# The tail of a two-layer convolution block: column sums moved between two matmuls, three loads moved earlier, two more load buffers

## The chip, the cores and the metric

The kernel runs on one core of a Trainium2 chip. The metric is the device time of a run in microseconds, the median of three timed runs. A profile of one more execution shows what each engine did: PE (matmuls; PEld is its weight load), DVE (vector work), ACT (activations), POOL (general work, and here also the issue of all indirect loads), SP (issue of most other transfers), and the 16 DMA engines that move the data for all queues.

## The reference

The input `x` is an image of 512 x 512 positions with 64 channels. Two layers are added to it, one after the other:

```
x = x + L0(group_norm(x))   # layer norm, gated triangular product over a mask, layer norm, output gate
x = x + L1(group_norm(x))   # 12 x 12 lowest Fourier modes, mixed over channels, transformed back
```

Only the end matters here. `group_norm` takes mean and variance over the whole image for 32 groups of two channels. `L1` needs the Fourier sums of the whole image at 12 x 12 modes; the norm's scale and shift are applied to the modes. Then, at each mode, a 64 x 64 complex matrix mixes the channels, and the inverse transform is added to every position. So nothing of the output can be finished before the last position of the first layer has been seen.

## The kernel before, in words

Only the path for a mask with at most 256 set rows (`compact`) runs. Rows are sorted so that masked ones stand together.

**The unit loop** (line 1047 on) makes the first layer's output `x1`. It goes over 32 units, each 32 columns x 256 rows of the image (two blocks r of 128 rows) in a buffer of 4096 values per partition (`place(i)`, a slice of the big tile `places`). Each unit has 8 steps n; in them PE transposes, centers and projects, DVE scales (`z_t`) and takes group statistics (`statistics`, L1023, into `stats2c`), ACT does sigmoids and squares, and POOL multiplies by the gate's partner (`gated`, L974) and adds to the input (`added`, L978). POOL also issues the loads of units to come (`load`, through `gather`, L628). All is emitted in this order by hand; each engine takes its instructions in the order of emission. The unit's results go to memory through SP (`store`, L994, to the halves `x1_h`, named `x_h` in the profile), its column sums go through `transform` and `save` (L1017) to `modes_d`. In the last unit but one SP issues the loads of the mixing weights `w_real` and `w_imag` (L1141) into `wide`, a part of `places`. The last quarter of the last unit is finished by DVE (`finished`) instead of POOL.

**Between the loops**, in order of emission: POOL clears `picks` (L1160), loads the last 128 rows of `modes_d` (`fetch(3)`, L893, into `modes_t`), and issues the loads of the first `AHEAD` = 13 tiles of `x1` (`fetch_rows`, L628). A tile is 128 rows x 32 columns x 64 channels, 1 MB; there are 64. Ten of the 13 buffers are parts of `places` that have come free, three are tiles `lx_t`. Then `group_norm_affine` computes scale and shift: a reduction on DVE, the matmul `mean_ps` (L253), four DVE steps up to `v`, the matmul `var_ps` (L265), and a chain of small DVE steps (`rsqrt` and what follows) up to `ab2`. After it `columns(3)` runs 12 matmuls `t_ps` (L888) over `modes_t` and adds the result to `sums` (L889). Then come `turned` (L1174), the writing of `picks`, the mixing matmuls `mixed_ps` (L1192), which read `picks` and `wide`, and the first `back_columns` (`q_ps`, `it_ps`), which makes a quarter of the inverse column transform.

**The last loop** (line 1246 on) takes the 64 tiles in order: four matmul groups `l_ps` (L1254), four additions on DVE (L1261), a store to the output through SP (L1262), and the load of the tile `AHEAD` places on into the same buffer, which waits until that store has landed. Three more `back_columns` are spread over it.

Of the kernel before, what the change touches and what calls it, by code (L numbers as in the profile page):

```python
# [9 lines left out]
F32 = mybir.dt.float32  # L10
# [7 lines left out]
P = 128  # L18
N = 512
C = 64  # L20
# [6 lines left out]
MODES = 12  # L27
M2 = 2 * MODES
EPS = 1e-5
JC = 32  # L30
NJ = N // JC
K = 2 * P
AHEAD = 13
SHARE = 22
QB = 4

# [10 lines left out]
def conv_preact_kernel(ctx: ExitStack, tc: tile.TileContext, t: dict):  # L47
# [190 lines left out]
        nc.vector.tensor_reduce(between, means, AX.X, ALU.add)  # L238
        nc.vector.scalar_tensor_tensor(var, var, 1.0 / count, between, ALU.mult, ALU.add)

    def group_norm_affine(keep, sets, each, name):


        groups, n = sets[0].shape[1:]
        avg = avg_p if groups == G else avg_c
        ab = keep.tile([P, 3], F32, name="ab_" + name)
        with tc.tile_pool(name="gn_" + name, bufs=1) as gp, tc.tile_pool(
            name="gnp_" + name, bufs=1, space=PSUM
        ) as gps:
            part = gp.tile([P, groups], F32, name="part")  # L250
            nc.vector.tensor_reduce(part, sets[0], AX.X, ALU.add)
            mean_ps = gps.tile([P, groups], F32, name="mean_ps")
            nc.tensor.matmul(mean_ps, avg, part, start=True, stop=True)  # L253
            mean = gp.tile([P, groups], F32, name="mean")
            nc.vector.tensor_scalar(mean, mean_ps, 1.0 / (n * each), None, ALU.mult)
            d = gp.tile([P, groups, n], F32, name="gn_d")
            nc.vector.scalar_tensor_tensor(
                d, sets[0], 1.0 / each, mean.unsqueeze(2).to_broadcast([P, groups, n]), ALU.mult, ALU.subtract
            )
            nc.vector.tensor_mul(d, d, d)  # L260
            nc.vector.scalar_tensor_tensor(d, sets[1], 1.0 / each, d, ALU.mult, ALU.add)
            v = gp.tile([P, groups], F32, name="v")
            nc.vector.tensor_reduce(v, d, AX.X, ALU.add)
            var_ps = gps.tile([P, groups], F32, name="var_ps")
            nc.tensor.matmul(var_ps, avg, v, start=True, stop=True)  # L265
            rs = rsqrt(gp, var_ps, 1.0 / n, EPS, [P, groups])
            if groups == G:
                mine = gp.tile([P, 2, G], F32, name="mine")
                nc.vector.tensor_mul(mine[:, 0, :], rs, pick)
                nc.vector.tensor_mul(mine[:, 1, :], mean, pick)  # L270
                am = gp.tile([P, 2], F32, name="am")
                nc.vector.tensor_reduce(am, mine, AX.X, ALU.add)
                rs, mean = am[:, 0:1], am[:, 1:2]
            nc.vector.scalar_tensor_tensor(ab[:, 1:2], mean, -1.0, rs, ALU.mult, ALU.mult)
            nc.vector.tensor_copy(ab[:, 0:1], rs)
            nc.vector.tensor_scalar(ab[:, 2:3], mean, -1.0, None, ALU.mult)
        return ab
# [334 lines left out]
    def compact(fc):  # L612
# [193 lines left out]
        with tc.tile_pool(name="tri", bufs=1) as trp:  # L806
# [57 lines left out]
            with tc.manual_schedule(), tc.tile_pool(name="late", bufs=1) as lp:  # L864
# [15 lines left out]
                parts = wide.rearrange("p a b -> p (a b)").rearrange("p (k f) -> p k f", k=2)  # L880
                modes_t = places[:, 7 * 64 * C : 7 * 64 * C + M2 * C].rearrange("p (m c) -> p m c", c=C)

                def columns(h, pool):
                    by = modes_t.rearrange("p (m k) c -> p m (k c)", k=2)
                    ps = pool.tile([P, 4, P], F32, name="t_ps").rearrange("p i k -> p (i k)")[:, : MODES * M2]
                    ps = ps.rearrange("p (m n) -> p m n", m=MODES)
                    for m in range(MODES):
                        nc.tensor.matmul(ps[:, m, :], by[:, m, :], col_basis[:, h, :], start=True, stop=True)  # L888
                    nc.vector.tensor_add(sums, sums, ps)  # L889

                def fetch(h):

                    (nc.gpsimd if h == 3 else nc.sync).dma_start(modes_t, modes_d[h * P : (h + 1) * P])  # L893

                with tc.tile_pool(name="np_x", bufs=LEAD + 2) as tp, tc.tile_pool(name="np_q", bufs=2) as sqp, tc.tile_pool(
                    name="np_s", bufs=3
# [150 lines left out]
                    for s in range(-LEAD, total_g + 2 * SIZE):  # L1047
# [94 lines left out]

                with tc.tile_pool(name="lq", bufs=1) as qp, tc.tile_pool(name="lx", bufs=1) as xp:

                    free = 3 * 64 * C + C * MODES * MODES
                    buffers = [places[:, free : free + JC * C].rearrange("p (n c) -> p n c", c=C)]
                    buffers += [place(i)[:, r * JC : (r + 1) * JC] for i in (6, 2, 0, 1) for r in range(2)]
                    buffers += [place(7)[:, JC:]]
                    buffers += [xp.tile([P, JC, C], F32, name=f"lx_t{i}") for i in range(AHEAD - len(buffers))]
                    ranked = [h.rearrange("s (k j) c -> (s k) (j c)", k=NJ // 2) for h in x1_h]  # L1150
                    tiles_left = [(jc, b) for jc in range(NJ) for b in range(4)]
                    xts = {}

                    def fetch_rows(jc, b):
                        xts[jc, b] = buffers[(4 * jc + b) % AHEAD]
                        gather(xts[jc, b].rearrange("p j c -> p (j c)"), ranked[jc // 8], dst_i, b, jc % 8)


                    picks = qp.tile([P, MODES, MODES, 32], F32, name="picks")
                    nc.gpsimd.memset(picks, 0.0)  # L1160
                    fetch(3)
                    for jb in tiles_left[:AHEAD]:
                        fetch_rows(*jb)
                    rinv = qp.tile([P, 4, P], F32, name="rinv")
                    nc.scalar.dma_start(rinv, t["c_rinv"])
                    col_inv = qp.tile([P, 2, 4, P], F32, name="col_inv")
                    nc.scalar.dma_start(col_inv, t["c_col_inv"])
                    ab2 = group_norm_affine(lp, sets, 8, "x1c")
                    with tc.tile_pool(name="tcp", bufs=1, space=PSUM) as tcp:
                        columns(3, tcp)  # L1170
                    with tc.tile_pool(name="sps", bufs=1, space=PSUM) as sps:

                        turned = sps.tile([P, MODES, M2], F32, name="turned")
                        nc.tensor.matmul(  # L1174
                            turned.rearrange("p m n -> p (m n)"), turn, sums.rearrange("p m n -> p (m n)"), start=True, stop=True
                        )
                        v = qp.tile([P, 2, MODES, MODES], F32, name="v_modes")
                        nc.vector.tensor_add(v[:, 0], sums[:, :, :MODES], turned[:, :, MODES:])
                        nc.vector.tensor_sub(v[:, 1], turned[:, :, :MODES], sums[:, :, MODES:])
                        for k in range(2):  # L1180
                            to = picks.rearrange("p m n k -> p m (n k)")[:, :, 12 * k : 12 * k + 33 * 11 + 1 : 33]
                            nc.vector.tensor_scalar(to, v[:, k], ab2[:, 0:1], None, ALU.mult)
                            h = slice(k * C, (k + 1) * C)
                            one = picks[h, 0, 0, 12 * k : 12 * k + 1]
                            nc.vector.scalar_tensor_tensor(one, ab2[h, 1:2], float(N * N), one, ALU.mult, ALU.add)

                        mixed_ps = sps.tile([P, 3, C], F32, name="mixed_ps")
                        for m3 in range(3):
# [54 lines left out]
                    with tc.tile_pool(name="lpq", bufs=1, space=PSUM) as pq, tc.tile_pool(  # L1243
                        name="lpt", bufs=2, space=PSUM
                    ) as pt, tc.tile_pool(name="lps", bufs=4, space=PSUM) as pp:
                        for jc in range(NJ):
                            for b in range(4):
                                it = parts[:, jc // 8, (jc % 8) * N : (jc % 8 + 1) * N]
                                xt = xts.pop((jc, b))
# [92 lines left out]
```

## Time and profile before

| | before |
|---|---|
| timed runs, us | 1892.57, 1892.95, 1894.03; median 1892.95 |
| the profiled execution: its own time, us | 1886.98 |
| its span, us | 1885.2 |
| busy in the span: PE, DVE, ACT, POOL | 89%, 77%, 49%, 46% |
| end of the statistics of the last unit, us | 1554.2 |
| end of the last mixing matmul, us | 1581.1 |
| DMA rate from 1602 to 1850 us | 425 GB/s |

Times in the text are counted from the start of the span. A line of a timeline gives the start, the time from there to the end of the group, the engine, the line of the kernel, the operation with its output and inputs, the number of instructions, and in brackets the idle time of the engine just before and what ended it. SPq, ACTq and POOLq are the issuing side of a queue. A line of the stretch table gives, for each stretch, its length, the busy time and the number of instructions of each engine, the granted TensorE clock as a share of full speed, the mean busy share of the DMA engines and the bytes that they moved per time. Shares slightly above 1 are an effect of how packets are counted into stretches.

### The profile page before, as it was taken

How to read it: one execution, taken by the hardware profiler on the slowest of the kernel's cores; microseconds unless marked ns; L12 is line 12 of the kernel's file. 1: busy time of each engine (PE TensorE's matmuls, PEld its weight loads, DVE VectorE, ACT ScalarE, POOL GpSimd, SP SyncE). 2: the span in 40 equal slices, each digit the busy share in tenths (PEclk: the TensorE clock that was granted, in tenths of full speed). 3: DMA queues.
4: the chain of work that ended last, by engine and by line, in shares of the span. 5: the costliest groups of instructions: out<-in, count | busy, mean ns of one | idle time of the engine just before them, and what ended most of it. 6: DMA issues, size and time to landing. Idle time of an engine off the chain costs nothing. (4 is left out here: it accounts for less than half of the span.)

```text
span 1885.2 us, 33737 instructions
## 1 busy us (share of the span) xinstructions
PE 1683.2 (89%) x11598; PEld 1350.9 (72%) x11598; DVE 1458.5 (77%) x2997; ACT 922.0 (49%) x1606; POOL 873.0 (46%) x678
## 2 busy tenths in 40 slices
PE   6779899998999999999999999999999956998873
PEld 5666666664788889998888888788888835664441
DVE  5989677777555568888999799979999994665552
ACT  3565555653222255567777677757767720111000
POOL 3655111111000000029999799979998982111110
PEclk9989899999999999999999899989999986555555
DMA  6999155556656534237777676767777589999999
GB/s 250 387 373 382 62 141 135 138 140 160 206 179 179 151 137 165 116 136 259 260 235 251 219 238 243 242 219 259 254 262 248 199 226 366 419 427 427 426 427 389
DMA packets 188868, 468.22 MB, mean 248 GB/s; under 512 B 35184, under 2 KB 134384, under 8 KB 147600
## 3 DMA queue, kind: packets, MB, share of 16 engines
q1 hardware_dynamic: 158192, 262.40, 41.4%
q0 software_dynamic: 27856, 202.19, 28.1%
q8 instruction: 94, 1.54, 0.3%
q10 hardware_dynamic: 2640, 1.38, 0.3%
q14 instruction: 86, 0.70, 0.1%
HBM read 278.13 MB, written 187.76 MB: 247 GB/s over the span
## 5 line engine op out<-in xcount | busy, mean ns | idle before, releaser
L934 PE MATMUL w_ps<-gate_x,xt_c 128*128 128x128 f32 x2048 | 281.9, 282 | 32.1 <-DVE z_t L1112 30.7
L978 POOL TENSOR_TENSOR places<-places,z_t 128x1024 f32<-128x1024 f32 x127 | 302.1, 2378 | 8.2
L934 PEld LDWEIGHTS w_ps<-gate_x,xt_c 128*128 128x128 f32 x2048 | 253.1, 195 | 49.1 <-DVE z_t L1112 48.6
L934 PE MATMUL c_ps<-center_x,xt_c 128*128 128x128 f32 x2048 | 276.3, 278 | 0.2
L934 PEld LDWEIGHTS c_ps<-center_x,xt_c 128*128 128x128 f32 x2048 | 252.5, 194 | 2.3 <-ACT xt_c L929 1.1
L944 ACT ACTIVATE sq_c<-c_ps 128x512 f32<-128x512 f32 x320 | 188.6, 590 | 104.3 <-PE c_ps L934 103.8
L1254 PE MATMUL l_ps<-places,rinv 24*128 24x512 f32 x512 | 209.7, 1128 | 31.7 <-DVE places L1261 25.7
L1112 DVE TENSOR_TENSOR z_t<-w_ps,rs_n 128x512 f32<-128x512 f32 x320 | 216.1, 675 | 23.0 <-PE w_ps L934 22.7
L1023 DVE BATCH_NORM_STATS2 stats2c<-places 128x6 f32<-128x128 f32 x1024 | 220.5, 279 | 8.1 <-POOL places L978 8.1
L948 DVE TENSOR_REDUCE scratch<-sq_c 128x16 f32<-128x1024 f32 x160 | 194.6, 1216 | 16.6 <-ACT sq_c L944 11.8
L1068 ACT ACTIVATE z_t<-z_t 128x1024 f32<-128x1024 f32 x128 | 135.5, 1058 | 142.0 <-DVE z_t L1115 117.7
L1115 DVE TENSOR_TENSOR z_t<-z_t,scratch 128x1024 f32<-128x1024 f32 x160 | 195.4, 1221 | 11.7 <-ACT rs_n L954 3.4
L1254 PEld LDWEIGHTS l_ps<-places,rinv 24*128 24x128 f32 x512 | 120.9, 304 | 115.4 <-DVE places L1261 73.1
L974 POOL TENSOR_TENSOR z_t<-z_t,bias_row_out 128x1024 f32<-128x1024 f32 x63 | 149.6, 2374 | 113.0 <-DMA places<-u_d 108.7
L924 PE MATMUL t_ps<-c_ident,places 128*128 128x128 f32 x1280 | 196.6, 277 | 1.3 <-DVE places L853 1.3
L1261 DVE TENSOR_TENSOR places<-places,l_ps 128x512 f32<-128x512 f32 x200 | 124.2, 683 | 86.5 <-DMA places<-x_h,dst_i 53.4
L929 ACT ACTIVATE xt_c<-t_ps,ab_xc 128x512 f32<-128x512 f32 x256 | 175.8, 687 | 23.8 <-PE t_ps L924 23.8
L924 PEld LDWEIGHTS t_ps<-c_ident,places 128*128 128x128 f32 x1280 | 148.9, 143 | 52.3 <-issue 52.3
L628 POOL DMA_INDIRECT places<-in_x,src_i x64 | 62.6, 978 | 261.9 <-PE c_ps L934 210.9
L974 POOL TENSOR_TENSOR z_t<-z_t,places 128x1024 f32<-128x1024 f32 x64 | 151.3, 2365 | 32.2 <-ACT z_t L1068 32.0
L678 DVE BATCH_NORM_STATS2 stats1c<-x_ps 128x6 f32<-128x512 f32 x256 | 156.0, 683 | 12.2 <-PE x_ps L677 11.3
L853 DVE SCALAR_TENSOR_TENSOR places<-tri_c_ps,slot_t,mask_s 128x256 f32<-128x256 f32 x128 | 73.1, 650 | 85.3 <-PE tri_c_ps L849 85.3
(203 smaller groups left out, 2641.9 us busy)
## 6 DMA issues: line engine op xcount, KB each, us to landing
x_h<-places SPq DMA_DIRECT2D x64, 1024.0 KB
out_x<-places SPq DMA_DIRECT2D x50, 1024.0 KB
places<-u_d SPq DMA_DIRECT2D x512, 64.0 KB
left_d<-o_c SPq DMA_DIRECT2D x64, 256.0 KB
right_d<-o_c SPq DMA_DIRECT2D x64, 256.0 KB
left_raw<-left_d SPq DMA_DIRECT2D x64, 256.0 KB
right_raw<-right_d SPq DMA_DIRECT2D x64, 256.0 KB
u_d<-z_t SPq DMA_DIRECT2D x32, 512.0 KB
```

The costliest lines, as they stand in the source:

```text
L678: nc.vector.bn_stats(stats[:, 0, 16 * (jc % quarter) + 4 * r + c, :], ps.rearrange("p i k -> p (i k)"))
L924: nc.tensor.transpose(tps[:, i, :], flat[:, o : o + P], ident)
L929: nc.scalar.activation(xts[s], tps, AF.Identity, bias=ab1[:, 2:3])
L934: nc.tensor.matmul(ps[:, 2 * i : 2 * i + 2, :], xts[s][:, i, :], w, start=True, stop=True)
L944: nc.scalar.activation(sqs[s // 2][:, 8 * (n % 2) : 8 * (n % 2) + 8, :], cps, AF.Square)
L948: nc.vector.tensor_reduce(totals[k % 2][:, 8 * (n - 1) : 8 * (n + 1)], sqs.pop(s // 2), AX.X, ALU.add)
L974: nc.gpsimd.tensor_mul(zs[k, c], zs[k, c], u)
L978: nc.gpsimd.tensor_add(xr, xr, zs.pop((k, c)))
L1023: nc.vector.bn_stats(st[k // 4][:, g, k % 4, :], x_of(k)[:, :, 2 * g : 2 * g + 2])
L1112: nc.vector.tensor_mul(z[:, 8 * odd : 8 * odd + 8, :], wps, rs)
L1115: nc.vector.tensor_add(z, z, bias.unsqueeze(1).to_broadcast([P, 16, C]))
L1254: nc.tensor.matmul(ps.rearrange("p j o -> p (j o)"), rinv[h, b, :], it[h], start=True, stop=True, tile_position=(32 * g, 0),)
```

## The change

It has three parts.

- `columns` is split into a list of steps. `group_norm_affine` gets a function `between`, which it calls after each of its two matmuls: seven of the twelve column matmuls are emitted right after `mean_ps`, five right after `var_ps`, and the addition to `sums` after the whole of `group_norm_affine`.
- The first three loads of the last loop's tiles are emitted inside the unit loop: one in the last unit but one at n = 3, two in the last unit at n = 3 and n = 6. There they stand on POOL after `gated` or `added` of that step.
- `AHEAD` is 15 instead of 13. The two added buffers are the memory of `picks`; their first loads are emitted after the mixing matmuls. The other ten of the first 13 loads stay where they were.

```diff
-AHEAD = 13
+AHEAD = 15
...
-    def group_norm_affine(keep, sets, each, name):
+    def group_norm_affine(keep, sets, each, name, between=lambda i: None):
...
             nc.tensor.matmul(mean_ps, avg, part, start=True, stop=True)
+            between(0)
...
             nc.tensor.matmul(var_ps, avg, v, start=True, stop=True)
+            between(1)
...
-                def columns(h, pool):
+                def column_sums(h, pool):
...
-                    for m in range(MODES):
-                        nc.tensor.matmul(ps[:, m, :], by[:, m, :], col_basis[:, h, :], start=True, stop=True)
-                    nc.vector.tensor_add(sums, sums, ps)
+                    steps = [
+                        lambda m=m: nc.tensor.matmul(ps[:, m, :], by[:, m, :], col_basis[:, h, :], start=True, stop=True)
+                        for m in range(MODES)
+                    ]
+                    return steps + [lambda: nc.vector.tensor_add(sums, sums, ps)]
...
+                buffers = [places[:, free : free + JC * C].rearrange("p (n c) -> p n c", c=C)]
+                buffers += [place(i)[:, r * JC : (r + 1) * JC] for i in (6, 2, 0, 1) for r in range(2)]
+                buffers += [place(7)[:, JC:]]
...
+                def fetch_rows(i):
+                    jc, b = tiles_left[i]
+                    fetched[jc, b] = buffers[i % AHEAD]
+                    gather(fetched[jc, b].rearrange("p j c -> p (j c)"), ranked[jc // 8], dst_i, b, jc % 8)
...
                             if n == 6:
                                 load(v + 3, 1)
+                        if (v, n) in ((last - 1, 3), (last, 3), (last, 6)):
+                            fetch_rows(len(fetched))
...
                     fetch(3)
-                    for jb in tiles_left[:AHEAD]:
-                        fetch_rows(*jb)
+                    buffers += [xp.tile([P, JC, C], F32, name=f"lx_t{i}") for i in range(AHEAD - 2 - len(buffers))]
+                    spare = picks.rearrange("p m n k -> p (m n k)")
+                    buffers += [spare[:, i * JC * C : (i + 1) * JC * C].rearrange("p (n c) -> p n c", c=C) for i in range(2)]
+                    for i in range(len(fetched), AHEAD - 2):
+                        fetch_rows(i)
...
-                    ab2 = group_norm_affine(lp, sets, 8, "x1c")
                     with tc.tile_pool(name="tcp", bufs=1, space=PSUM) as tcp:
-                        columns(3, tcp)
+                        steps = column_sums(3, tcp)
+
+                        def some(i):
+                            for step in steps[7 * i : 7 * i + 7 - 2 * i]:
+                                step()
+
+                        ab2 = group_norm_affine(lp, sets, 8, "x1c", some)
+                        steps[-1]()
...
+                        for i in range(AHEAD - 2, AHEAD):
+                            fetch_rows(i)
...
                                 ahead = 4 * jc + b + AHEAD
                                 if ahead < len(tiles_left):
-                                    fetch_rows(*tiles_left[ahead])
+                                    fetch_rows(ahead)
```

More of the change, by code (lines that the diff above doesn't have):

```diff
@@ L886, in columns @@
                     ps = ps.rearrange("p (m n) -> p m n", m=MODES)
-                    for m in range(MODES):
-                        nc.tensor.matmul(ps[:, m, :], by[:, m, :], col_basis[:, h, :], start=True, stop=True)
-                    nc.vector.tensor_add(sums, sums, ps)
+                    steps = [
[3 more added lines that the diff above has]
+                    return steps + [lambda: nc.vector.tensor_add(sums, sums, ps)]
+                def columns(h, pool):
+                    for step in column_sums(h, pool):
+                        step()
                 def fetch(h):
                     (nc.gpsimd if h == 3 else nc.sync).dma_start(modes_t, modes_d[h * P : (h + 1) * P])
+                free = 3 * 64 * C + C * MODES * MODES
+                buffers = [places[:, free : free + JC * C].rearrange("p (n c) -> p n c", c=C)]
+                buffers += [place(i)[:, r * JC : (r + 1) * JC] for i in (6, 2, 0, 1) for r in range(2)]
+                buffers += [place(7)[:, JC:]]
+                ranked = [h.rearrange("s (k j) c -> (s k) (j c)", k=NJ // 2) for h in x1_h]
+                tiles_left = [(jc, b) for jc in range(NJ) for b in range(4)]
+                fetched = {}
+                def fetch_rows(i):
+                    jc, b = tiles_left[i]
+                    fetched[jc, b] = buffers[i % AHEAD]
+                    gather(fetched[jc, b].rearrange("p j c -> p (j c)"), ranked[jc // 8], dst_i, b, jc % 8)
                 with tc.tile_pool(name="np_x", bufs=LEAD + 2) as tp, tc.tile_pool(name="np_q", bufs=2) as sqp, tc.tile_pool(
@@ L1143, in compact @@
                 with tc.tile_pool(name="lq", bufs=1) as qp, tc.tile_pool(name="lx", bufs=1) as xp:
[L1145 to L1156, printed above, removed]
                     picks = qp.tile([P, MODES, MODES, 32], F32, name="picks")
@@ L1167, in compact @@
                     nc.scalar.dma_start(col_inv, t["c_col_inv"])
-                    ab2 = group_norm_affine(lp, sets, 8, "x1c")
                     with tc.tile_pool(name="tcp", bufs=1, space=PSUM) as tcp:
-                        columns(3, tcp)
+                        steps = column_sums(3, tcp)
+                        def some(i):
+                            for step in steps[7 * i : 7 * i + 7 - 2 * i]:
+                                step()
+                        ab2 = group_norm_affine(lp, sets, 8, "x1c", some)
+                        steps[-1]()
                     with tc.tile_pool(name="sps", bufs=1, space=PSUM) as sps:
@@ L1248, in compact @@
                                 it = parts[:, jc // 8, (jc % 8) * N : (jc % 8 + 1) * N]
-                                xt = xts.pop((jc, b))
+                                xt = fetched.pop((jc, b))
                                 group = []
```

## The prediction

> **What bounds the kernel now.** I began with the chain of work that ended last, on the page: a transfer of the output ends it, and matmuls take a small part.
>
> ```profile
> DMA 10%; PE 5%; DVE 1%; issue 0%; ACT 0%; POOLq 0%; SPq 0%; DVEq 0%; ACTq 0%
> ```
>
> Next the table of stretches of the tail, for the DMA share (second column from the right):
>
> ```profile
> core 0: us, PE busy (x) PEld busy (x) DVE busy (x) ACT busy (x) POOL busy (x), PEclk, DMA share, GB/s
> 1511.50:1538.50 27.00, 18.73 (x118) 13.43 (x119) 24.42 (x65) 8.97 (x10) 24.80 (x11) 0.93 0.99 225
> 1538.50:1545.00 6.50, 3.65 (x12) 0.78 (x11) 6.07 (x18) 2.11 (x2) 6.34 (x4) 0.76 1.02 429
> 1545.00:1554.00 9.00, 2.08 (x8) 0.34 (x8) 9.00 (x43) 0.59 (x1) 6.13 (x4) 0.50 0.50 169
> 1554.00:1591.00 37.00, 22.05 (x354) 19.27 (x354) 13.76 (x43) 4.29 (x6) 11.93 (x13) 0.66 1.00 398
> 1591.00:1595.50 4.50, 3.74 (x15) 2.26 (x16) 3.00 (x5) 0.00 (x0) 0.00 (x0) 0.70 0.31 129
> 1602.00:1850.00 248.00, 208.57 (x561) 126.05 (x558) 143.25 (x231) 20.05 (x24) 46.82 (x50) 0.50 1.01 425
> 1850.00:1881.00 31.00, 7.73 (x16) 3.96 (x16) 6.90 (x12) 0.00 (x0) 0.00 (x0) 0.50 1.00 420
> ```
>
> From 1602 to 1881 the DMA engines are full. So the end of the kernel is the first store of the output plus the transfers that are still to be made then, and nothing that PE or DVE do after 1602 matters. Ahead of it the DMA has two holes: 1545 to 1554 (half idle, 4.5 us) and 1591 to 1595.5 (3.1 us). In the second, all 13 loads have landed and no tile has been finished.
>
> When does the first store leave? The timelines of POOL, DVE, PE and SP show the serial path to it (start, length, engine, line):
>
> ```profile
> 1475.17 2.37 POOL L978 TENSOR_TENSOR places<-places,z_t 128x1024 f32<-128x1024 f32 x1
> 1477.69 0.98 POOL L628 DMA_INDIRECT places<-in_x,src_i  x1 [0.15 <-issue]
> 1478.69 2.38 POOL L974 TENSOR_TENSOR z_t<-z_t,bias_row_out 128x1024 f32<-128x1024 f32 x1
> ...
> 1541.54 2.37 POOL L974 TENSOR_TENSOR z_t<-z_t,bias_row_out 128x1024 f32<-128x1024 f32 x1
> 1543.99 2.34 POOL L978 TENSOR_TENSOR places<-places,z_t 128x1024 f32<-128x1024 f32 x1
> 1546.27 3.94 POOL L1160 MEMSET picks<- 128x4608 f32 x1
> 1552.78 0.59 POOL L893 DMA_DIRECT2D places<-modes_d  x1 [2.56 <-DMA modes_d<-places]
> ```
> ```profile
> 1546.41 7.82 DVE L1023 BATCH_NORM_STATS2 stats2c<-places 128x6 f32<-128x128 f32 x40
> ```
> ```profile
> 1557.83 0.61 PE L253 MATMUL mean_ps<-part,c_avg_p 128*128 128x32 f32 x2 [9.37 <-DVE part L251]
> 1560.59 0.63 PE L265 MATMUL var_ps<-v,c_avg_p 128*128 128x32 f32 x2 [2.15 <-DVE v L263]
> 1561.50 5.32 PE L888 MATMUL t_ps<-col_basis,places 128*128 128x24 f32 x24 [0.28 <-DVE rq_v L199]
> 1568.36 1.33 PE L1174 MATMUL turned<-sums,turn 128*128 128x288 f32 x2 [1.54 <-DVE sums L889]
> ```
> ```profile
> 1594.63 3.19 SPq L1262 DMA_DIRECT2D out_x<-places  x2
> ```
>
> POOL's last addition ends at 1546.33 and DVE's last statistics start at 1546.41, with nothing between: POOL sets that start. Then it is a chain of single steps up to `turned`, the mixing of the modes, the first `back_columns`, and the first store at 1594.63.
>
> **Two more buffers.** Before the first store 15 tiles can be loaded instead of 13. A tile is 1.049 MB; at the 425 GB/s of 1602 to 1850 that is 2.47 us, so two take **4.9 us** out of the work that stands behind the first store. This counts if they land in the holes. The memory of the picks comes free when the last `mixed_ps` matmul ends (1581.12 before); the DMA then still has the earlier loads to move, so its 1 us of issue is covered. From 1554 to 1595.5 the DMA worked 37.0 + 0.31 x 4.5 = 38.4 us. With three tiles moved ahead of it (7.4) and two added (4.9) it is 35.9 us; from 1556.2 (below) it ends at 1592.1, ahead of the first store. If the early loads filled no hole, it would end at about 1599; the hole at 1591 would still be filled, and 3.1 us of the 4.9 be gained. Steady state and drain are at share 1.0 either way, and more buffers add no work there.
>
> **Three early loads.** Each puts one L628 on POOL. The row above gives its price there: the start-to-start of L978 and L974 around it is 3.52 us, without it 2.31 to 2.44; other pairs with a load give 3.50. So 1.07 to 1.21 us each. The first follows the product of the last-but-one unit, at 1513.5; POOL idles 1.69 us before 1522.54 waiting for ACT's sigmoid, which covers it (uncovered: 1.2). The second and third follow 1534.4 and 1541.6, where POOL runs without a gap up to 1546.33, and their cost goes straight to the statistics: 2 x 1.15 less 0.08 of slack, **2.2 us later** (2.0 to 2.4). The memset, the wait for `modes_d` and the ten other loads behind them on POOL move as much. The transfers compete with the weight loads (full from 1511.5 to 1538.5) and push the stores of the last units into the hole at 1545; the weights are wanted only at 1571, and the buffers that wait for those stores only from about 1558. That is why I take them at nothing. If the pushed stores hold up the four writes of `modes_d`, its load is late; before, it had landed by 1557.46, 1.0 us ahead of the end of the mean's matmul, so about 1 us is covered.
>
> The Trainium skill (SBUF — State Buffer, A bandwidth-pool intuition that's wrong, and Who interferes with whom) speaks against loads from POOL beside a busy DVE: writing the descriptors waits while DVE holds a shared port, 620 ns becoming 3100. By that, as an estimate, five times 0.98 us for each of three loads, less the cover, is 13.0 us of delay and 5.4 us slower in the end; the operations that it names (copy, tensor_scalar) are not those on DVE from 1533 to 1546. The trace decides for the low price: 64 loads issued amid DVE work took 936 to 1010 ns (median 981), against a median of 936 for those of the last stage.
>
> **Column sums.** Call M the end of the mean's matmul (1558.45). Before, `turned` starts at M + 9.91. The 12 steps are 24 records in 5.32 us, 0.44 each, and 1.0 us more until DVE may read them. Now seven stand between mean and variance: 3.1 us, where DVE needs 2.1 for `v`; so `var_ps`, queued behind them on PE, starts at M + 3.1 instead of M + 2.14, and DVE waits 1 us for it. From there 0.65 for the matmul and 2.9 for the root and the affine (1561.23 to 1564.14); the other five steps (2.2 + 1.0) end inside this. Then the sum's addition, 0.45: `turned` at M + 7.2, **2.7 us earlier**. Nearest rows either way: 3.0 if the steps start in the drain of the mean, 1.7 if the modes land 1 us after M.
>
> **Sum.** First store: +2.2 - 2.7 = -0.5 us. Work behind it: -4.9. Together -5.4. The profiled execution took 1886.98 us (span 1885.2 and 1.8 around it), so 1881.6 and a span of 1879.8. The median of the timed runs, 1892.95, stands 6.0 above the profiled execution; I keep this distance: **1887.5 us**. A measurement of this kernel can tell about 0.2%, 3.8 us.
>
> **Rivals.**
> *Gain eaten on the way to the first store.* The granted clock was 0.50 from 1545 until the mixing had run for 4 us, then 1.00 for most of 1575.7 to 1592.8. If the moved matmuls shift this, `q_ps` and `it_ps` run at half clock as in the second call: 16 records in 3.3 instead of 1.8 us, and 3.9 instead of 3.3, 2.1 us together. With it 1889.6; with the modes late as well, 1890.6. If only the hole at 1591 is filled, 3.1 + 0.5: 1889.4. All inside 0.2%. For it: share 0.99 where the early loads land. Against: the mixing starts at nearly the same time.
> *Slower: the early loads stall POOL.* In the last stage L628 waited 24 times for stores, 95.1 us, 4.0 each. If the three loads wait likewise for room, each costs 5.1; less the cover of 1.7 and 0.1, the statistics are 13.5 late and the first store 10.8, so 10.8 - 4.9 = 5.9 us slower: 1898.9. It decides from 7.6 us of delay. Against: in the changed program's instruction list the three carry no semaphore wait, and the previous load from POOL was issued 36 us earlier.
> *Does not do what it says.* The two buffers start too late or the DMA's total is not what ends the kernel: then -0.5, 1892.5. Against: share 1.01 for 250 us.
>
> **How the numbers follow.** Forecast 0.70, with a range of its own from 1886.2 to 1888.9 (unknown costs of 1 us and 0.7 of run to run): faster. Eaten gain 0.18 and nothing 0.04: the same, 0.22. Slower 0.08. The range from 1886.2 to 1891.0 holds the forecast and the eaten gain; outside are 0.12 and the tails.
>
> **What would show it.** Right: two L628 between 1534 and 1545 and the statistics at about 1548.6; `t_ps` as 14 and 10 records, `turned` 7.2 us after the mean; two loads into the picks at about 1581; DMA share near 1 from 1511 to 1554; first store near 1594.1; full DMA to the end. Wrong: a first store later than 1597, or idle DMA after 1602.

## The result and the profile after

| | before | after |
|---|---|---|
| median of the timed runs, us | 1892.70 (22 runs, on the same chip) | 1890.57 (22 runs) |
| ratio, with its 95% interval | | 0.9988 (0.9979 to 0.9997) |
| the profiled execution: its own time, span, us | 1886.98, 1885.2 | 1891.34, 1889.6 |

The gain is 2.1 us, about 0.1%, where 5.4 were forecast. The interval just leaves out 1, but a second measurement of the same kernel, among the experiments, gave 1.0008 (0.9991 to 1.0024), so whether anything is gained stays open. The time lies in the range given, near its upper end, but not by the path forecast.

The two profiled executions can't be laid on each other by the start of the span. Both programs are the same up to the last two units, and yet the one of after reaches them 3.8 us later. So I count from a **mark**: the start of POOL's first product `z_t` (`gated`) in the last unit but one, 1511.13 in before and 1514.89 in after. "At 35.1" below means 35.1 us after the mark.

The timeline of POOL after, around the end of the unit loop (start, time to the end of the group, engine, line, operation, count, idle time before):

```profile
1544.05 2.35 POOL L1002 TENSOR_TENSOR places<-places,z_t 128x1024 f32<-128x1024 f32 x1
1546.55 0.98 POOL L630 DMA_INDIRECT places<-x_h,dst_i  x1
1547.54 2.37 POOL L998 TENSOR_TENSOR z_t<-z_t,bias_row_out 128x1024 f32<-128x1024 f32 x1
1549.99 2.35 POOL L1002 TENSOR_TENSOR places<-places,z_t 128x1024 f32<-128x1024 f32 x1
1552.27 3.94 POOL L1172 MEMSET picks<- 128x4608 f32 x1
1563.30 0.59 POOL L902 DMA_DIRECT2D places<-modes_d  x1 [7.09 <-DMA modes_d<-places]
```

The early load costs 0.98 us, as forecast, and the memset stands at 37.4 where it stood at 35.1. But look at the last line: POOL waited 2.56 us for the four writes of `modes_d` before and waits 7.09 now. The load of the modes is issued at 48.4 and not at 41.7. Next ACT, which issues those writes; DVE; and PE, where `t_ps` needs the loaded modes:

```profile
1555.10 1.98 ACTq L1041 DMA_DIRECT2D modes_d<-places  x4
```
```profile
1550.16 1.64 DVE L1047 BATCH_NORM_STATS2 stats2c<-places 128x6 f32<-128x128 f32 x8
1552.37 6.27 DVE L1047 BATCH_NORM_STATS2 stats2c<-places 128x6 f32<-128x128 f32 x32 [0.57 <-POOL places L1002]
```
```profile
1562.25 0.61 PE L253 MATMUL mean_ps<-part,c_avg_p 128*128 128x32 f32 x2 [7.92 <-DVE part L251]
1569.11 3.18 PE L891 MATMUL t_ps<-col_basis,places 128*128 128x24 f32 x14 [6.25 <-DMA places<-modes_d]
1572.11 0.61 PE L266 MATMUL var_ps<-v,c_avg_p 128*128 128x32 f32 x2
1572.54 2.31 PE L891 MATMUL t_ps<-col_basis,places 128*128 128x24 f32 x10
1576.09 1.33 PE L1195 MATMUL turned<-sums,turn 128*128 128x288 f32 x2 [1.24 <-DVE ab_x1c L277]
```

The writes were all issued by 1557.1, but POOL learns of their landing only at 1563.3. `t_ps` waits 6.25 us for the load, and `var_ps`, which now stands behind it on PE, waits with it. The statistics are hardly late: the 40 instructions have come apart, eight of them run while POOL still adds, and the last one ends at 43.75 against 43.1.

The table of stretches after shows where the DMA is full and where it isn't (second column from the right):

```profile
core 0: us, PE busy (x) PEld busy (x) DVE busy (x) ACT busy (x) POOL busy (x), PEclk, DMA share, GB/s
1552.00:1557.50 5.50, 1.94 (x8) 0.20 (x8) 5.13 (x27) 0.58 (x1) 4.22 (x2) 0.50 1.02 427
1557.50:1561.00 3.50, 0.00 (x0) 0.00 (x0) 2.79 (x10) 0.64 (x2) 0.00 (x0) 0.50 0.95 389
1561.00:1566.00 5.00, 0.61 (x2) 0.50 (x2) 2.85 (x8) 0.00 (x0) 2.09 (x3) 0.50 0.76 230
1566.00:1597.50 31.50, 20.83 (x348) 18.62 (x348) 8.52 (x30) 2.63 (x3) 9.94 (x11) 0.66 1.00 410
1597.50:1603.50 6.00, 4.14 (x15) 2.05 (x15) 2.88 (x5) 1.01 (x1) 0.00 (x0) 0.50 0.13 55
1602.00:1850.00 248.00, 211.52 (x586) 131.12 (x586) 152.80 (x246) 20.03 (x24) 45.88 (x49) 0.51 1.00 419
```

The hole at 1545 of before is filled (1.02 and 0.95 from 1552 to 1561), but for 1.2 us just behind (0.76 from 1561 to 1566). The hole ahead of the first store isn't gone: it has grown from 3.1 to 6.0 x 0.87 = 5.2 us, because the first store leaves at 1603.42, which is 88.5 after the mark and not 83.5. What was saved in one hole is idle in the other. From the mark to 99 us behind it the DMA's idle time, added up from the packet records, is 9.2 us against 9.7 before.

### The profile page after: what moved, and what is told of

It reads as the page before. It is cut to its first block, busy times and chain, and to the rows that moved or that the text cites. A ratio compares the mean times of both kernels' runs of the same rounds, so it can differ in the third digit from the quotient of the medians.

```text
span 1889.6 us, 33738 instructions
## 1 busy us (share of the span) xinstructions
PE 1679.6 (89%) x11598; PEld 1351.0 (71%) x11598; DVE 1458.7 (77%) x2997; ACT 922.3 (49%) x1606; POOL 873.4 (46%) x678
## 4 chain that ended last, share of the span: by engine, by line
PE 52%; DVE 15%; DMA 14%; POOL 7%; issue 5%; ACT 3%; SPq 2%; POOLq 1%; ACTq 0%; DVEq 0%
PE c_ps L958 9%; PE w_ps L958 8%; PE tri_c_ps L851 7%; DMA out_x<-places 6%; PE t_ps L948 4%; PE l_ps L1277 4%; PE sides_c L748 3%; PE cc_ps L717 3%; POOL z_t L998 3%; DVE stats2c L1047 3%; PE gates_c L748 3%; DVE scratch L972 3%; DVE z_t L1138 3%; PE x_ps L679 2%; DVE z_t L1141 2%
## 5 line engine op out<-in xcount | busy, mean ns | idle before, releaser
L958 PEld LDWEIGHTS w_ps<-gate_x,xt_c 128*128 128x128 f32 x2048 | 253.2, 195 | 46.7 <-DVE z_t L1138 46.5
L1277 PE MATMUL l_ps<-places,rinv 24*128 24x512 f32 x512 | 204.8, 1114 | 28.5 <-DVE places L1284 16.7
L1284 DVE TENSOR_TENSOR places<-places,l_ps 128x512 f32<-128x512 f32 x176 | 110.1, 682 | 75.3 <-PE l_ps L1277 41.0
```

The costliest lines, as they stand in the source:

```text
L958: nc.tensor.matmul(ps[:, 2 * i : 2 * i + 2, :], xts[s][:, i, :], w, start=True, stop=True)
L1277: nc.tensor.matmul(ps.rearrange("p j o -> p (j o)"), rinv[h, b, :], it[h], start=True, stop=True, tile_position=(32 * g, 0),)
```

## The experiments

All of them go by the marks. The table gives, in us after each run's mark: the end of the statistics; when the stores of the last units had landed and when the last of the 256-byte writes of `modes_d` had (both from the packet records); the issue of the load of the modes; `t_ps`; `turned`; the first store of the output; and the end of the span. The last column is the ratio to before with its interval.

| run | stats end | stores landed | writes landed | modes load | t_ps | turned | first store | end | ratio |
|---|---|---|---|---|---|---|---|---|---|
| before | 43.1 | 38.9 | 41.0 | 41.7 | 50.4 | 57.2 | 83.5 | 374.1 | 1 |
| after | 43.8 | 46.7 | 47.5 | 48.4 | 54.2 | 61.2 | 88.5 | 374.7 | 0.9988 (0.9979 to 0.9997) |
| after_2 | 43.8 | 46.3 | 47.1 | 47.9 | 54.2 | 61.2 | 89.1 | 375.6 | 1.0008 (0.9991 to 1.0024) |
| e_cols | 43.1 | 38.9 | 41.1 | 41.8 | 47.1 | 54.3 | 80.2 | 372.1 | 0.9996 (0.9978 to 1.0015) |
| e_early | 43.8 | 47.1 | 47.8 | 48.7 | 55.1 | 61.0 | 88.5 | 379.5 | 1.0025 (1.0005 to 1.0044) |
| e_noearly | 43.1 | 38.9 | 41.0 | 41.7 | 47.1 | 54.1 | 80.4 | 368.5 | 0.9972 (0.9953 to 0.9992) |
| e_free | 42.2 | 38.0 | 40.1 | 40.7 | 46.2 | 53.2 | 80.5 | 366.7 | 0.9972 (0.9954 to 0.9991) |
| e_two | 43.1 | 43.7 | 44.4 | 45.3 | 52.1 | 59.0 | 86.8 | 373.8 | 0.9998 (0.9985 to 1.0012) |
| e_ballast | 43.1 | 46.0 | 46.7 | 47.9 | 54.5 | 60.3 | 86.7 | 377.9 | 1.0025 (1.0008 to 1.0041) |
| e_order | 43.8 | 40.8 | 43.1 | 44.0 | 49.6 | 56.7 | 82.8 | 370.8 | 0.9975 (0.9955 to 0.9995) |
| e_fill | 42.2 | 38.0 | 40.1 | 40.8 | 47.1 | 55.4 | 81.8 | 367.7 | 0.9985 (0.9966 to 1.0004) |
| e_noearly_2 | 43.1 | 39.0 | 41.0 | 41.7 | 47.1 | 57.1 | 84.7 | 371.5 | 0.9968 (0.9950 to 0.9986) |
| e_free_2 | 42.2 | 38.4 | 40.1 | 40.7 | 46.2 | 56.3 | 83.2 | 369.1 | 0.9970 (0.9949 to 0.9990) |

The theory: the three early tiles take up the DMA engines ahead of the last units' stores, the writes of `modes_d` come through only as those stores drain, and all that follows from the modes is late. The rivals: the new order of PE is the fault (`var_ps` behind `t_ps`); the issue of the loads on POOL is the fault; the two buffers are worth nothing.

**e_cols: the column sums alone.** The changed kernel without the early loads and without the added buffers.

```diff
-AHEAD = 15
+AHEAD = 13
...
-                        if (v, n) in ((last - 1, 3), (last, 3), (last, 6)):
-                            fetch_rows(len(fetched))
...
-                        for i in range(AHEAD - 2, AHEAD):
-                            fetch_rows(i)
```

> Column sums between the two matmuls alone: no early loads, 13 buffers. Two marks, both counted from the start of POOL's first product of the last unit but one: first store (before 83.5 us, changed 88.5) and the end of the span (before 374.1, changed 374.7). Late modes (the four small writes of modes_d share the DMA engines with stores that the early loads pushed back, and everything that needs the modes waits): nothing is pushed here, POOL waits 2.6 us for modes_d as before, turned starts 7.2 us after the mean's matmul, first store 80.8, end 371.4, ratio of times 0.9986. Rival, the order on PE (var_ps behind seven column matmuls costs what was lost): turned no earlier than the 9.9 us of before, first store 83.5 or later, ratio 1.000 or more.

The timeline of PE in e_cols:

```profile
1564.33 0.61 PE L253 MATMUL mean_ps<-part,c_avg_p 128*128 128x32 f32 x2 [9.37 <-DVE part L251]
1564.75 3.16 PE L891 MATMUL t_ps<-col_basis,places 128*128 128x24 f32 x14
1567.73 0.61 PE L266 MATMUL var_ps<-v,c_avg_p 128*128 128x32 f32 x2
1571.88 1.32 PE L1191 MATMUL turned<-sums,turn 128*128 128x288 f32 x2 [1.42 <-DVE sums L894]
```

With the modes there in time nothing waits between the mean and the variance. `turned` starts 6.9 us after the end of the mean's matmul (7.2 forecast, 9.91 before), 3.0 us earlier by the marks, and the first store 3.3 us earlier. So the order on PE is not the fault. In the time this does not show (1889.20 against 1889.31 us): the interval takes in both 0 and 3.3 us, so the run leaves open how much of a sooner first store comes through without more buffers.

**e_early: the early loads alone.** The changed kernel with 13 buffers and the column sums behind the norm, as before.

```diff
-AHEAD = 15
+AHEAD = 13
...
-                        ab2 = group_norm_affine(lp, sets, 8, "x1c", some)
-                        steps[-1]()
+                        ab2 = group_norm_affine(lp, sets, 8, "x1c")
+                        columns(3, tcp)
...
-                        for i in range(AHEAD - 2, AHEAD):
-                            fetch_rows(i)
```

> The three early loads alone: columns after the norm as before, 13 buffers. Late modes: POOL waits about 7 us for modes_d instead of 2.6, the column matmuls start about 4 us later than before (counted from the same mark), first store 87.4 to 88.5, end 378 to 379, ratio 1.002 to 1.0026. Rival, only the price of two issues on POOL: POOL waits 2.6 us for modes_d, first store 85.7, end 376.3, ratio 1.0012.

The early loads by themselves make the kernel slower: 1893.90 against 1889.31 us, the first store 5.0 us later. It is the delay of after, 88.5, to the tenth, although here `var_ps` is not behind `t_ps`. Against after the end is 4.8 us later with the same first store. That is the worth of the two buffers, of which this kernel has none.

**e_noearly and e_free: the change without early loads, and with two that stand ahead of the busy stretch.** The first has no early loads; the second makes two, in the third-last unit and at the start of the last but one, into two buffers that are free by then.

```diff
-                        if (v, n) in ((last - 1, 3), (last, 3), (last, 6)):
-                            fetch_rows(len(fetched))
```
```diff
-                buffers = [places[:, free : free + JC * C].rearrange("p (n c) -> p n c", c=C)]
+                buffers = [place(7)[:, JC:], places[:, free : free + JC * C].rearrange("p (n c) -> p n c", c=C)]
...
-                buffers += [place(7)[:, JC:]]
...
-                        if (v, n) in ((last - 1, 3), (last, 3), (last, 6)):
+                        if (v, n) in ((last - 2, 6), (last - 1, 1)):
```

> The change without its three early loads: columns between the matmuls and 15 buffers. Late modes: POOL waits 2.6 us for modes_d, first store 80.8, the loads run without a gap into the first stores (the hole of 3 us is filled), end 370 to 371, ratio 0.998. Rival, the two buffers bring nothing: end as for the columns alone, 371.4 or later, with idle DMA ahead of the first store.

> Columns between the matmuls, 15 buffers, and two early loads at other places: one in the last unit but two after n = 6, into the upper half of place 7, which the unit loop does not use, one in the last unit but one at n = 1; none in the last unit. The DMA engines are idle for 8.5 us there before, so the loads should push nothing. Late modes: POOL waits 2.6 to 3.6 us for modes_d, first store 81 to 82, end 367.5 to 369, ratio 0.997. Rival, the order on PE or POOL's issue costs it anyway: first store 85 or later, ratio 1.000.

Both are faster than before: 1884.41 and 1883.48 us against 1889.31. The changed kernel was not timed beside them; its two ratios, 0.9988 and 1.0008, lie above theirs (0.9972), though the first interval overlaps. The stretches of e_noearly, from the first loads to the first store at 1594.80, the last 3.5 us of that by themselves, and after it:

```profile
1557.00:1594.50 37.50, 23.98 (x362) 20.47 (x364) 16.21 (x48) 4.27 (x6) 14.07 (x15) 0.68 0.99 397
1591.00:1594.50 3.50, 2.61 (x12) 1.40 (x14) 2.21 (x4) 0.08 (x1) 0.00 (x0) 0.82 1.03 428
1594.50:1602.00 7.50, 7.50 (x24) 5.18 (x22) 6.66 (x11) 0.00 (x0) 0.00 (x0) 0.50 1.01 425
```

The two tiles in the picks fill the hole ahead of the first store (share 1.03 where before had 0.31), which needed no early load. Against e_cols the end is 3.6 us earlier with the same first store.

POOL in e_free, and the stretch in which its first load is moved and the second begins to be:

```profile
1500.64 0.98 POOL L630 DMA_INDIRECT places<-x_h,dst_i  x1
...
1510.35 0.98 POOL L630 DMA_INDIRECT places<-x_h,dst_i  x1 [0.27 <-POOL z_t L997]
...
1554.40 0.60 POOL L902 DMA_DIRECT2D places<-modes_d  x1 [2.53 <-DMA modes_d<-places]
```
```profile
1501.00:1514.00 13.00, 11.40 (x97) 9.99 (x96) 12.74 (x31) 9.30 (x14) 11.32 (x7) 1.00 0.59 204
```

With the loads in it the share of this stretch is 0.59, and POOL's wait for `modes_d` stays at 2.53. The end is 1.8 us earlier than in e_noearly by the marks, but these two loads lie ahead of the mark, so what their issue costs POOL isn't in that figure; the times of the two can't be told apart.

**after_2: the changed kernel again**, beside the next three, no edit.

> The changed kernel once more, for a second profile of its tail: is the lateness of the modes there every time? Late modes: POOL waits 6.5 to 7.5 us for modes_d again, first store 88 to 89 us after POOL's first product of the last unit but one, end of the span 374 to 375.5 after it (before 374.1), ratio 0.998 to 1.001. Rival, the profiled execution was an unlucky one: the wait is 2.6 to 4 us, first store 81 to 84, end 369 to 371.

Its marks repeat those of after within 0.6 us, 0.9 us at the end. Its time is 1890.49 against 1889.99 us.

**e_ballast: the transfers without the loads.** The kernel before, with three transfers of a tile's size added on SP where the weights are loaded. They write values of a finished unit to memory that nobody reads. POOL issues nothing more than before; the three stand in SP's own queue.

```diff
+        extra_d = dram.tile([3, P, JC * C], F32, name="extra_d")
...
+                            for i, (k2, r) in enumerate(((last - 2, 0), (last - 2, 1), (last - 2, 0))):
+                                nc.sync.dma_start(
+                                    extra_d[i], x_of(k2)[:, r * JC : (r + 1) * JC].rearrange("p j c -> p (j c)")
+                                )
```

> The kernel before, with three more stores of 1 MB on SP's queue just ahead of the weight loads: they write rows of a finished unit to a scratch tensor that nothing reads. No load from POOL is moved, columns and buffers are as before. It puts 7.4 us of other work in front of the last unit's stores, as the three early loads do. Late modes: POOL's memset stays at 35.1 us, its wait for modes_d grows from 2.6 to 6 to 8 us, first store 87 to 88.5, end 377.5 to 379.5 (before 374.1), ratio 1.002. Rival, the loads on POOL themselves (their issue, or their place in the queue ahead of the modes' load) make the modes late: wait 2.6 to 3 us, first store 83.5, end 374 to 375.

POOL, ACT's issue and PE in e_ballast:

```profile
1548.19 3.94 POOL L1165 MEMSET picks<- 128x4608 f32 x1
1560.97 0.59 POOL L894 DMA_DIRECT2D places<-modes_d  x1 [8.84 <-DMA rinv<-in_c_rinv]
```
```profile
1551.06 1.88 ACTq L1018 DMA_DIRECT2D modes_d<-places  x4
```
```profile
1567.56 5.29 PE L889 MATMUL t_ps<-col_basis,places 128*128 128x24 f32 x24 [4.47 <-DMA places<-modes_d]
```

The memset and the statistics stand where they stood before (35.1, 43.1), and still POOL waits 8.84 us ahead of the load of the modes and issues it 6.3 us late (6 to 8 us of wait were forecast). (The profile names a later small transfer of ACT's queue that landed at nearly the same time; the last of the writes had landed at 46.7, as the table says.) So neither the issue on POOL nor the loads' being loads is needed for the delay: three tiles of transfers ahead of the stores are enough. The time is 3.8 us above before: nothing of the change is there to give it back.

**e_two: two early loads** instead of three.

```diff
-                        if (v, n) in ((last - 1, 3), (last, 3), (last, 6)):
+                        if (v, n) in ((last - 1, 3), (last, 3)):
```

> The change without the third early load (two early loads, 15 buffers, columns between the matmuls). Late modes: 2.5 us less is pushed, so POOL's wait for modes_d is 4 to 5.5 us, first store 84 to 86, end 370 to 372.5, ratio 0.998. Rival, the third load alone does the harm (it is the last in POOL's queue ahead of the modes' load): wait 2.6 to 3 us, first store 81, end 368.5.

Here I missed. I expected a smaller delay from two tiles, with a first store of 84 to 86 and an end of 370 to 372.5; they came at 86.8 and 373.8, and the time is that of before. Two tiles push the stores from 38.9 to 43.7, so 4.8 us for 2 x 2.47, and the modes by 3.6. The third load adds 3.1 to the stores and as much to the modes.

**e_order: the last unit's stores moved out of the way.** All of the change is kept, early loads too; the two stores of the last unit are issued by POOL behind the load of the modes instead of by SP in the unit loop.

```diff
-                    def store(k, r):
+                    def store(k, r, queue=nc.sync):
...
-                        if n == 6 and v - 1 == last:
-                            for r in range(2):
-                                store(last, r)
...
                     fetch(3)
+                    for r in range(2):
+                        store(last, r, nc.gpsimd)
```

> The change with one edit: the two stores of the last unit are issued by POOL right behind the load of the modes, instead of by SP ahead of it. The three early loads stay. Late modes: the 2 MB that stood beside the writes of modes_d are gone, so POOL waits 3 to 5 us for them instead of 7.1, first store 82.5 to 86, end 368.5 to 372, ratio 0.997 to 0.998. Rival, the early loads or their issue on POOL hold up the modes, not the stores: wait 6 us or more, first store 88 or later, end 374 or later.

POOL in e_order:

```profile
1546.99 3.94 POOL L1169 MEMSET picks<- 128x4608 f32 x1
1553.60 0.59 POOL L902 DMA_DIRECT2D places<-modes_d  x1 [2.66 <-DMA modes_d<-places]
```

The wait is back at 2.66 us and the first store at 82.8, with the three early loads still in place: 1883.32 against 1889.99 us. The transfers that held up the writes were SP's last stores, pushed by the early loads. (In the table, 40.8 is when the stores that SP still issues had landed.) This is a third version that is faster than before; after_2, timed beside it, took 1890.49 us.

**e_big: larger packets for the last modes.** To see whether the writes lose for being 256 bytes each, the last 32 rows of `modes_d`, which the four writes carry, are written into a memory of their own in pieces of 2 KB per partition (96 packets instead of 768), and the load of the modes becomes five.

```diff
-                            queue.dma_start(modes_d[o : o + 8].rearrange("j m c -> m j c"), ft[32 * g : 32 * g + M2])
+                            if jc == NJ - 1:
+                                queue.dma_start(modes_l[g].rearrange("m j c -> m (j c)"), ft[32 * g : 32 * g + M2].rearrange("m j c -> m (j c)"))
+                            else:
+                                queue.dma_start(modes_d[o : o + 8].rearrange("j m c -> m j c"), ft[32 * g : 32 * g + M2])
```

> The change with the last four writes of the modes as 24 packets of 2 KB each, into a tensor of their own, instead of 192 of 256 B; POOL then loads 96 rows from modes_d and four times 8 rows from the new tensor (four more issues, of up to 1 us each). The three early loads and the pushed stores stay. If many small packets that take turns with packets of 8 KB make the modes late: the four writes, issued about 40.2 us after the mark, have landed by 43 to 45 (48.4 in the changed kernel). Rival, the writes just come after the bytes that stand ahead of them on the engines, whatever their packets: landed at 47 or later. First store 85 to 87 in the first case, since the added issues take back some 3 us, and 90 or later in the second.

The first and the last of POOL's four loads from the new memory:

```profile
1563.87 0.69 POOL L908 DMA_DIRECT2D places<-modes_l  x1 [3.64 <-DMA modes_l<-places]
...
1568.46 0.63 POOL L908 DMA_DIRECT2D places<-modes_l  x1 [1.09 <-DMA rinv<-in_c_rinv]
```

The idea that larger packets would do falls: of the four loads, which wait each for its write, the first is issued at 45.5, while SP's stores still run (to 47.5), but the last at 50.1, later than the single load of after. By the signs written down it is the rival that was met: the last write had landed at 49.8, and the first store left at 90.6. But its reason, that the writes just come behind all bytes ahead of them, doesn't fit the first write, which had landed at 45.2. The kernel is slower than before: 1897.65 against 1892.45 us, ratio 1.0024 (1.0012 to 1.0036). What the records say of it is in the last section.

**e_fill: one more load into the hole at the end of the unit loop.** e_free with one tile more, issued just ahead of the load of the modes.

```diff
+                    fetch_rows(len(fetched))
                     fetch(3)
```

> The version with early loads at free places (first store 80.5 us after the mark, end 366.7), and one more load issued by POOL between its memset and its load of the modes, into a buffer that has come free: it fills part of the 4 us in which the DMA engines are idle around the writes of the modes, but its 8 KB packets stand beside these writes. Late modes: the wait for modes_d grows by 1 to 2.5 us on top of the issue, and about 1 us of it is covered, so first store 81 to 82.5, end 365.5 to 368, ratio 0.997. Rival, a load beside the writes costs them nothing: first store 80.5, end 364.5 to 365.5, ratio 0.996.

The load of the modes is issued as in e_free (40.8), but it now shares the DMA with a tile: `t_ps` is 0.9 us later, `turned` 2.2 and the first store 1.3. Of the 2.2 us, 1.0 is a wait of the addition to `sums` that comes up again below. The longer wait for `modes_d` that I forecast didn't come, but the run doesn't test a load beside the writes: the tile's first packet moved at 40.1, when the last write landed. The time is 1887.20 against 1892.45 us, and the interval takes in 1.

**e_noearly_2 and e_free_2: the two best once more, beside each other.** No new edit.

> The change without its early loads once more: marks 80.4 and 368.5, tail 5.6 us shorter, ratio 0.9965 to 0.998. Rival, as above: 0.999.

> The version with its two early loads at free places once more, to see whether its gain holds: by its marks (first store 80.5, end 366.7 against 374.1 before) the tail is 7.4 us shorter, ratio 0.996 to 0.9975. Rival, the first measurement was luck and the gain is that of the columns alone: ratio 0.999.

Against 1891.70 us for before they took 1884.97 and 1886.76: ratios 0.9968 (0.9950 to 0.9986) and 0.9970 (0.9949 to 0.9990). The marks did not repeat: the first stores came at 84.7 and 83.2 where 80.4 and 80.5 were expected, the ends at 371.5 and 369.1. Up to `t_ps` the profiles agree with the first ones. Then DVE's addition to `sums` starts late, in e_noearly_2:

```profile
1567.51 0.46 DVE L894 TENSOR_TENSOR sums<-sums,t_ps 128x288 f32<-128x288 f32 x1 [2.91 <-remote]
```

The wait is 2.9 us here, 2.8 in e_free_2, 1.5 in e_big and 1.0 in e_fill, and in none of the other runs; what ended it the profile doesn't name. These four ran on other chips than the rest of the experiments. The cause stays open, and so does whether before would have the wait there too. The single profiles of e_noearly and e_free are thus good to some 3 us behind `t_ps`; the times hold.

The simplest of the versions, the change without early loads, is 5 to 7 us faster than before, about as much as e_free and e_order, and none of the three can be told from the others.

## Why the prediction was right in its range and wrong in its path

That the time fell into the range is luck. The gain forecast, 5.4 us, didn't come. The rival with late modes has 1890.6 us, next to the 1890.57 measured, but from other terms: it adds 3.1 us ahead of the first store, and 5.5 came there (5.0 late instead of 0.5 early). In the profiles the tail of after ends 0.6 us later than that of before, not 2.3 earlier as that rival has it.

**The step that failed** is that of the early loads' transfers: "That is why I take them at nothing." The text saw that they "push the stores of the last units into the hole at 1545", asked who waits for that, and allowed 1 us for it. It took the cover from when the modes had landed before, and left out that the writes of `modes_d` themselves come through only as the stores end. That is shown by e_ballast and e_order, not by the trace of before; with it, the sum comes out of that trace: stores landed at 38.9, and three tiles at 2.47 us make 46.3 (measured 46.7); the writes, held up at least to there, can land no sooner than that (47.5), and the load behind them was issued at 48.4 and not at 41.7. It landed at 54.2, where `t_ps` starts, instead of 46.3. Of these 7.9 us, 4.0 were cover in the old order, in which `t_ps` started only at 50.4. So `turned` came 4.0 us late, where with the column sums moved and the modes there in time it comes 3.0 us early (e_cols).

**The last 1.0 us of the delay** lies between `turned` and the first store, and goes with the clock, as the first rival had it, but in another place. In before the first eight matmuls `l_ps` still ran at the clock of 1.00:

```profile
1589.40:1592.80 3.40, 1.61 (x12) 0.54 (x10) 1.69 (x3) 1.22 (x2) 0.00 (x0) 1.00 0.83 347
```
```profile
1590.97 1.14 PE L1254 MATMUL l_ps<-places,rinv 24*128 24x512 f32 x8 [1.10 <-ACT places L1238]
```

After, at 0.50 (the row from 1597.5 above), they take nearly twice as long:

```profile
1598.81 2.09 PE L1277 MATMUL l_ps<-places,rinv 24*128 24x512 f32 x8 [1.10 <-ACT places L1261]
```

**Two more buffers: right.** Forecast 4.9 us; measured 3.6 us between e_cols and e_noearly and 4.8 between e_early and after, both at nearly equal first stores, with one profile of each.

**Column sums: right where the modes are on time.** Forecast 2.7, measured 3.0 (e_cols) and 3.1 (e_noearly). In e_noearly_2 and e_free_2 the wait ahead of `sums` takes most of it away (`turned` at 57.1 and 56.3). In after nothing of it is left, since `t_ps` waits.

**The early loads on POOL: price right, effect mis-sized.** 0.98 us each, and the memset 2.2 us later, as forecast; but the statistics end 0.65 us later, not 2.2. The slack was not the 0.08 us between POOL's last addition and DVE's statistics: eight of the 40 statistics don't need that addition and now run ahead of it. The term that I priced was the small one.

**The sum.** Forecast: first store -0.5, work behind it -4.9. Measured: +5.0 and -4.4 (end +0.6). So the outcome is that of the rival "gain eaten on the way to the first store", modes late, though by 6.8 us and not by one. The rival in which POOL stalls falls: none of the loads waited. The document's own sign of failure, a first store later than 1597, came true: 1603.4, or 1599.7 counted from the mark of before.

## What to carry to other kernels

A transfer that is moved earlier doesn't only fill a hole: it pushes what comes behind it on the DMA engines, here by about its own length (4.8 us for two tiles, 7.8 for three), so list the small transfers on which a serial chain waits, and let the large ones beside them go behind, as e_order does. Early loads did no harm where the DMA engines had room for them (share 0.59 in e_free, the loads included), and did at the edge of a full stretch (0.99) with the hole behind it; that they gain anything beyond the buffers the times don't show. And before early issue is used to fill a hole, look at whether more buffers fill the one that counts without it: in e_noearly they did.

## What was not expected of the hardware

How small writes fare beside large stores. In e_ballast ACT issued the four writes of `modes_d` from 38.0 to 39.9, just as in before, and they landed at 46.7 instead of 41.0. Over the thirteen rows of the table the last of them landed 0.7 to 2.2 us behind the stores each time, wherever between 38.0 and 47.1 that was.

The packet records of after show how. The 768 writes of 256 bytes take 0.018 us each, a store's packet of 8 KB 0.31 us. From 43.5 to 45.5 both queues are served, and 71 writes pass beside 99 store packets. The writes go over 12 engines (in before each of the four ends with 12 semaphore packets) and the stores over 16, so that is 5.9 writes and 6.2 store packets for an engine: one small packet for each large one. From 46.0 to 46.5, with the stores nearly gone, 334 pass. Each engine has 64 of them, and at 0.34 us a turn (2 / 5.9) they would take 22 us, so most of them pass only when the stores end. With 2 KB packets (e_big) each of the four writes leaves an engine two packets and a semaphore, three turns of 0.31 us, and the semaphores of the first three began to come 1.1 and 1.2 us apart. The fourth landed at 49.8, 2.3 us behind the stores, with packets of POOL's loads on the engines too; what held it up isn't shown. Besides, the first write passes 3.4 us after its issue in after, e_ballast and e_big, and 0.8 us after it in before, where the stores were ending.

The Trainium skill (DMA: Bandwidth & Descriptors, Queues, rings and completion order) says that each DMA engine takes turns between the queue rows that have work, a packet at a time, and gives a packet as some 9 to 17 descriptors. The turns agree with these records, the size of a turn doesn't: it was one 256-byte write here. It would also explain why POOL's loads lose nothing beside SP's stores: with 8 KB in a packet on both sides they had 0.50 and 0.51 of the engines from 1610 to 1850 in after. Taking turns is read from the records alone; no run changed it by itself, and writes issued by POOL or SP instead of ACT weren't tried.
